# Recurrence: four of seven groups turned by DMA in pairs of tiles, eps added on VectorE, another order within a slot

## The chip, the cores and the metric

The kernel runs on one core of one Trainium2 chip. The metric is the device time of one execution in microseconds. The kernel before took 1867.72 us in the median of 3 runs (1865.54 to 1868.72).

## The reference, cut to what matters

There are 3327 rows of 256 values. Two graph attention layers and a mixture of experts come first, and then a recurrence of 30 steps over all rows. The change lies in the recurrence alone:

```python
def step(h, _):
    h = h + 0.01 * jnp.tanh(h)
    h = h * jax.nn.sigmoid(h)
    h = _layernorm(h, ln_w, ln_b)
    h = jnp.einsum('bsc,dc->bsd', h, W) + b
    return (h, None)
x, _ = jax.lax.scan(step, x, None, length=N_ITERS)     # N_ITERS = 30
...
x = x + _L1_ffn_ref((_layernorm(x, axis=-1))[None], ...)[0]
```

Each row goes through its 30 steps on its own; no row needs another. All of it is in float32.

## The kernel before

The rows lie in on-chip memory (SBUF) as 26 tiles of 128 rows by 256 values, `x`. In the recurrence the tiles are worked in seven groups: groups 0 to 5 have four tiles, group 6 has two. A "group" in the code is one group in one step, counted on through all steps, so `at` runs from 0 to 209, `at % 7` is the group and `at // 7` the step. Below, "group 3" means `at % 7 == 3`.

Within one step a group passes through these stages, each a method of the class `Group`:

- `tanh` (L1050, ScalarE): tanh of the state, one instruction for the group.
- `add` (L1053, GpSimd, called POOL in the profile): adds the state to it, one instruction, both operands in SBUF.
- `silu` (L1057, ScalarE): writes `z`.
- `measure` (VectorE, DVE in the profile): per tile the statistics (`bn_stats`, L1062) and their aggregate (`bn_aggr`, L1065), which give the variance.
- `invert` (GpSimd): adds eps to the variance (L1070) and raises it to the power -1/2 (L1071), 128 by 4 values.
- The turning of `z`: the product takes it with the 256 features along the partitions. `turn_here` does it on TensorE: two transposes for each tile (L1081) into PSUM, and a ScalarE copy for each pair of tiles out of PSUM (L1083). `turn_away` does it by DMA, on 16-bit halves: a ScalarE copy splits each float into its two halves (L1090, `parts`), a DMA writes them to DRAM (L1091, `apart`), and a transposing DMA reads them back (L1095, `zTa`). Both DMAs are issued by SyncE (SP). Groups 1, 3 and 5 go away, the others are turned here.
- `product` (TensorE, L1105): two matrix products for each tile against the 256x256 weight `wc`, into PSUM (`po`, two buffers). The profile shows each product as two MATMUL records.
- `evict` (VectorE, L1115): scales by the inverse deviation, adds the bias, and writes the new state, one instruction for each tile. One of its inputs lies in PSUM, the other, `bb`, in SBUF. In the last step it also adds the state kept from before the recurrence (L1122 loads it, L1123 adds it) and sends the rows out.

The loop at the end of the kernel is a software pipeline written out by hand. One turn of it is called a slot here. In a slot, group `at` is multiplied, while groups ahead of it pass through earlier stages; from the second step on the order of the instructions within each engine is exactly the order of the calls. Each engine works its own queue in order, so what a call waits for holds up what comes after it on that engine only.

```python
for at in range(-6, LAST + 2):
    on(at - 1, Group.evict)
    live.pop(at - 1, None)
    on(at + 3, Group.invert)
    on(at + 4, Group.silu)
    on(at + 2, lambda g: g.away or g.turn_here())
    on(at + 4, lambda g: g.away and g.turn_away())
    on(at + 4, Group.measure)
    on(at + 6, Group.tanh)
    on(at + 5, Group.add)
    on(at, Group.product)
```

So in one slot VectorE evicts group `at - 1` and measures group `at + 4`; GpSimd inverts `at + 3` and adds `at + 5`; ScalarE does silu and, for a group that goes away, `parts` of `at + 4`, or the copies of `at + 2`, and then tanh of `at + 6`; TensorE transposes `at + 2` and multiplies `at`. The tanh of `at + 6` needs the eviction of `at - 1` (the same rows, one step earlier) from the same slot. Buffers: `th` 3, `z` 4, `zT` 2, `parts` and `zTa` 2 each, DRAM `apart` 2.

The first attention layers use a large matrix of edges in SBUF, `adjT`, which is read for the last time (L281, VectorE, two SBUF inputs) just before the recurrence. Some of the recurrence's first stages for the first groups run beside that second attention stage.

Of the kernel before, what the change touches and what calls it, by code (L numbers as in the profile page):

```python
# [11 lines left out]
F32 = mybir.dt.float32  # L12
I32 = mybir.dt.int32
I16 = mybir.dt.int16
BF16 = mybir.dt.bfloat16
FP8 = mybir.dt.float8e4
AF = mybir.ActivationFunctionType
ALU = mybir.AluOpType
# [3 lines left out]
P = 128  # L22
ALPHA = 0.2
EPS = 1e-5
N_STEPS = 30
S = 100.0
G = 4
# [4 lines left out]
def gat_moe_gat_recurrent_ffn(ctx: ExitStack, tc: tile.TileContext, a: dict, out: bass.AP):  # L32
    nc = tc.nc
    N, D = a["x"].shape
    KD = D // P
    NT = (N + P - 1) // P
    NP = NT * P
    PAIRS = NT // 2
# [145 lines left out]
    class Scores:  # L184


        def __init__(self, pool, heads, s=None):
            self.s = pool.tile([P, NT, 2, heads], F32, name="s") if s is None else s
            self.row = pool.tile([P, NT, heads], F32, name="row")
            self.full = pool.tile([P, NT, heads], F32, name="full")  # L190
            self.part = pool.tile([P, NT, heads], F32, name="part")
            self.minus = pool.tile([P, NT, heads], F32, name="minus")
# [113 lines left out]
    graph = ctx.enter_context(tc.tile_pool(name="graph", bufs=1))  # L306
    adj_pairs = graph.tile([P, PAIRS, NP], BF16, name="adjT")
    adjT = adj_pairs.bitcast(FP8).rearrange("p c (i b) -> p c i b", b=2)
# [37 lines left out]
    dram = ctx.enter_context(tc.tile_pool(name="dram", bufs=1, space=bass.MemoryType.DRAM))  # L346
# [35 lines left out]
    with ExitStack() as moe:  # L382
# [447 lines left out]
        def product(hT, w):  # L830

            p = bank().rearrange("p (f q) -> p f q", f=FH)
            for f in range(FH):
                for k in range(KD):
                    nc.tensor.matmul(  # L835
                        p[:, f, :], lhsT=w[:, k, f * P : (f + 1) * P], rhs=hT[:, k, :],
                        start=(k == 0), stop=(k == KD - 1),
                    )
            return p
# [108 lines left out]
    narrow = ctx.enter_context(tc.tile_pool(name="narrow", bufs=8))  # L948
# [74 lines left out]
    with ExitStack() as st:  # L1023
        ps_t = st.enter_context(tc.tile_pool(name="ps3t", bufs=2, space=PSUM))
        turns = cycle((ps, ps_t))
        ps_o = st.enter_context(tc.tile_pool(name="ps3o", bufs=2, space=PSUM))
        last_p = st.enter_context(tc.tile_pool(name="last", bufs=2))

        apart = [dram.tile([G * P, 2, D], I16, name=f"apart{q}") for q in range(2)]
        apart_p = st.enter_context(tc.tile_pool(name="apart", bufs=2))  # L1030

        AWAY = (1, 3, 5)
        COUNT = len(groups)
        LAST = N_STEPS * COUNT

        class Group:

            def __init__(self, at):
                self.at = at
                self.ts = groups[at % COUNT]  # L1040
                self.n = len(self.ts)
                self.hs = x[:, self.ts[0] : self.ts[0] + self.n, :]
                self.away = at % COUNT in AWAY and at > 1

            def put(self, ins):
                return tc.keep_in_program_order(ins) if self.at >= COUNT else ins

            def tanh(self):
                self.th = steps["th"].tile([P, G, D], F32, name="th")[:, : self.n, :]
                self.put(nc.scalar.activation(self.th, self.hs, AF.Tanh, scale=1.0 / S))  # L1050

            def add(self):
                self.put(nc.gpsimd.tensor_tensor(self.th, self.th, self.hs, ALU.add))  # L1053

            def silu(self):
                self.z = steps["z"].tile([P, G, D], F32, name="z")[:, : self.n, :]
                self.put(nc.scalar.activation(self.z, self.th, AF.Silu, scale=1.0 / S))  # L1057

            def measure(self):
                stats = narrow.tile([P, G, 6], F32, name="stats")  # L1060
                for j in range(self.n):
                    self.put(nc.vector.bn_stats(stats[:, j, :], self.z[:, j, :]))  # L1062
                self.v = narrow.tile([P, G, 2], F32, name="v")
                for j in range(self.n):
                    self.put(nc.vector.bn_aggr(self.v[:, j, :], stats[:, j, :]))  # L1065

            def invert(self):
                self.r = narrow.tile([P, G], F32, name="rr")
                r = self.r[:, : self.n]
                self.put(nc.gpsimd.tensor_scalar(r, self.v[:, : self.n, 1], EPS, None, op0=ALU.add))  # L1070
                self.put(nc.gpsimd.tensor_tensor(r, r, neg_half[:, : self.n], ALU.pow))  # L1071

            def turn_here(self):
                pool = next(turns)
                zT = steps["zT"].tile([P, G, KD, P], F32, name="zT")
                for c in range(self.n // 2):
                    pt = pool.tile([P, 2, KD, P], F32, name="bank")
                    for j in range(2):
                        for k in range(KD):
                            (tc.keep_in_program_order if self.at > 1 else lambda ins: ins)(  # L1080
                                nc.tensor.transpose(pt[:, j, k, :], self.z[:, 2 * c + j, k * P : (k + 1) * P], ident)  # L1081
                            )
                    self.put(nc.scalar.copy(zT[:, 2 * c : 2 * c + 2, :, :], pt))  # L1083
                self.zT = lambda j, k: zT[:, j, k, :]

            def turn_away(self):
                n = self.n
                parts = apart_p.tile([P, G, 2, D], I16, name="parts")[:, :n]
                here = apart[self.at % COUNT // 2 % 2][: n * P]
                self.put(nc.scalar.copy(parts, self.z.bitcast(I16).rearrange("p j (d b) -> p j b d", b=2)))  # L1090
                nc.sync.dma_start(  # L1091
                    here.rearrange("(j p) b d -> p j (b d)", p=P), parts.rearrange("p j b d -> p j (b d)")
                )
                zT = apart_p.tile([P, KD, G * P], F32, name="zTa")
                nc.sync.dma_start(  # L1095
                    zT.bitcast(I16)[:, :, : n * 2 * P], here.rearrange("t b d -> (t b) d"), transpose=True
                )
                self.zT = lambda j, k: zT[:, k, j * P : (j + 1) * P]

            def product(self):  # L1100
                self.po = ps_o.tile([P, G, D], F32, name="po")
                for j in range(self.n):
                    for k in range(KD):
                        tc.keep_in_program_order(
                            nc.tensor.matmul(  # L1105
                                self.po[:, j, :], lhsT=self.zT(j, k), rhs=wc[:, k, :],
                                start=(k == 0), stop=(k == KD - 1),
                            )
                        )

            def evict(self):
                ts, n = self.ts, self.n
                for j in range(n):
                    self.put(
                        nc.vector.scalar_tensor_tensor(  # L1115
                            self.hs[:, j, :], self.po[:, j, :], self.r[:, j : j + 1], bb, op0=ALU.mult, op1=ALU.add
                        )
                    )
                if self.at >= LAST - COUNT:
                    here = slice(ts[0] * P, (ts[-1] + 1) * P)  # L1120
                    old = last_p.tile([P, G, D], F32, name="old")
                    nc.sync.dma_start(old[:, :n, :], kept[here, :].rearrange("(t p) d -> p t d", p=P))  # L1122
                    nc.vector.scalar_tensor_tensor(  # L1123
                        self.hs, self.hs, 1.0 / S, old[:, :n, :], op0=ALU.mult, op1=ALU.add
                    )
                    move_pairs(out, self.hs, ts[0] // 2, (ts[-1] + 1) // 2, True)

        live = {}

        def on(at, *what):  # L1130
            if 0 <= at < LAST:
                if at not in live:
                    live[at] = Group(at)
                for w in what:
                    w(live[at])

        for at in range(-6, LAST + 2):
            on(at - 1, Group.evict)
            live.pop(at - 1, None)
            on(at + 3, Group.invert)  # L1140
            on(at + 4, Group.silu)
            on(at + 2, lambda g: g.away or g.turn_here())
            on(at + 4, lambda g: g.away and g.turn_away())
            on(at + 4, Group.measure)
            on(at + 6, Group.tanh)
            on(at + 5, Group.add)
            on(at, Group.product)


# [47 lines left out]
```

## Time and profile before

| | us |
|---|---|
| median of 3 runs | 1867.72 |
| profiled execution, whole | 1862.0 |
| its span | 1860.3 |
| second attention stage: start of its last matmul (L286) | 1082.9 |
| recurrence, steady steps | 25.51 to 25.52 each |
| stretch from the start of the last step's products (1826.89) to the end | 33.41 |

The page gives busy time for each engine over the whole span (PE is TensorE's matmul, PEld its weight load, DVE VectorE, ACT ScalarE, POOL GpSimd). Inside the recurrence these shares are different from those of the whole, so the stretch of one step has to be asked for by itself. Durations of one instruction in the recurrence, from the groups by line between 1140 and 1820 us:

| line | engine | what | mean ns |
|---|---|---|---|
| L1050 | ACT | tanh, four tiles / two | 1060 / 639 |
| L1053 | POOL | add, four tiles / two | 2366 / 1278 |
| L1057 | ACT | silu, four tiles / two | 1052 / 613 |
| L1062 | DVE | statistics, one tile | 413 |
| L1065 | DVE | aggregate, one tile | 155 |
| L1070 | POOL | eps, four tiles | 229 |
| L1071 | POOL | power, four tiles / two | 1038 / 716 |
| L1083 | ACT | copy of two turned tiles | 576 |
| L1090 | ACT | parts of four tiles | 1900 |
| L1115 | DVE | evict, one tile | 475 |

Instructions of one engine overlap at their ends, so two in a row take less than the sum: four evictions take 1.66 us together, four statistics 1.41 us.

The longest waits in the same stretch, over its 26.6 steps, are all short: ScalarE's silu for GpSimd's add 69.1 us in 106 waits (longest 1.6), VectorE's eviction for TensorE 60.8 us in 106 (longest 1.1) and for GpSimd's `rr` 35.4 us in 27 (longest 1.3). TensorE has no wait in the list.

### The profile page before, as it was taken

How to read it: one execution, taken by the hardware profiler on the slowest of the kernel's cores; microseconds unless marked ns; L12 is line 12 of the kernel's file. 1: busy time of each engine (PE TensorE's matmuls, PEld its weight loads, DVE VectorE, ACT ScalarE, POOL GpSimd, SP SyncE). 2: the span in 40 equal slices, each digit the busy share in tenths (PEclk: the TensorE clock that was granted, in tenths of full speed). 3: DMA queues.
4: the chain of work that ended last, by engine and by line, in shares of the span. 5: the costliest groups of instructions: out<-in, count | busy, mean ns of one | idle time of the engine just before them, and what ended most of it. 6: DMA issues, size and time to landing. Idle time of an engine off the chain costs nothing.

```text
span 1860.3 us, 32198 instructions
## 1 busy us (share of the span) xinstructions
PE 1809.2 (97%) x11212; PEld 1653.9 (89%) x11212; DVE 1284.7 (69%) x3829; ACT 1186.9 (64%) x1498; POOL 939.3 (50%) x864
## 2 busy tenths in 40 slices
PE   7999999999999998899999999999999999999997
PEld 6999999998999998688888888888888888888886
DVE  7888888852222222666776778888888888888887
ACT  2877777641111111556666678888888888888884
POOL 3010212255333331101111159999999999999994
PEclk9999999999999999999999999999999999999999
DMA  8898260169999885400000035554555455555557
GB/s 175 114 122 99 57 100 22 61 224 298 339 338 336 298 284 166 151 14 17 21 15 17 17 108 125 124 127 125 118 132 117 123 133 125 121 121 125 125 127 202
DMA packets 377309, 253.97 MB, mean 137 GB/s; under 512 B 238821, under 2 KB 336924, under 8 KB 377146
## 3 DMA queue, kind: packets, MB, share of 16 engines
q1 hardware_dynamic: 361026, 219.04, 43.1%
q0 software_dynamic: 11440, 28.09, 8.8%
q10 hardware_dynamic: 4680, 4.76, 0.8%
q8 instruction: 91, 1.49, 0.3%
q14 instruction: 72, 0.59, 0.1%
HBM read 168.19 MB, written 76.49 MB: 132 GB/s over the span
## 4 chain that ended last, share of the span: by engine, by line
PE 67%; issue 10%; DVE 6%; POOL 5%; DMA 5%; ACT 0%; SPq 0%; POOLq 0%; DVEq 0%; ACTq 0%
PE po L1105 35%; PE acc L286 24%; PE bank L1081 5%; DVE pT L281 3%; POOL given L855 2%; POOL rb L761 2%; DMA given<-wh,to 2%; DMA wh<-in_w_dram 1%; DMA old<-kept 1%; DMA lists<-pair,ati 1%; PE bank L835 1%; PE acc L163 1%; PE bank L526 1%; POOL rstd L121 1%; PE bank L148 0%
## 5 line engine op out<-in xcount | busy, mean ns | idle before, releaser
L276 ACT ACTIVATE e<-rb,minus,full 128x384 f32<-128x384 f32 (+3 forms) x494 | 400.1, 823 | 166.7 <-DVE pT L281 150.6
L1053 POOL TENSOR_TENSOR th<-th,x 128x1024 f32<-128x1024 f32 (+1 forms) x210 | 465.1, 2215 | 16.0 <-ACT th L1050 14.4
L281 DVE SCALAR_TENSOR_TENSOR pT<-e,part,adjT 128x384 f32<-128x384 f32 (+3 forms) x494 | 383.3, 780 | 118.8 <-PE acc L286 103.4
L1115 DVE SCALAR_TENSOR_TENSOR x<-po,rr,bb 128x256 f32<-128x256 f32 x780 | 323.0, 475 | 104.2 <-PE po L1105 67.3
L1105 PE MATMUL po<-wc,zT 128*128 128x256 f32 x1696 | 385.9, 379 | 1.2 <-DVE x L1115 1.2
L1105 PEld LDWEIGHTS po<-wc,zT 128*128 128x128 f32 x1696 | 315.1, 190 | 40.7 <-issue 1.6
L1105 PE MATMUL po<-wc,zTa 128*128 128x256 f32 x1424 | 321.9, 379 | 0.0
L286 PE MATMUL acc<-wh,pT 128*128 128x129 f32 x2704 | 309.8, 276 | 2.1 <-DVE pT L281 2.1
L286 PEld LDWEIGHTS acc<-wh,pT 128*128 128x128 f32 x2704 | 305.0, 192 | 2.7 <-DVE pT L281 2.5
L1105 PEld LDWEIGHTS po<-wc,zTa 128*128 128x128 f32 x1424 | 268.3, 190 | 35.3
L286 PE MATMUL acc<-s_wh,pT 128*128 128x257 f32 x1352 | 295.2, 381 | 3.5 <-DVE pT L281 3.3
L286 PEld LDWEIGHTS acc<-s_wh,pT 128*128 128x128 f32 x1352 | 256.0, 190 | 42.1 <-DVE pT L281 6.3
L1062 DVE BATCH_NORM_STATS2 stats<-z 128x6 f32<-128x256 f32 x780 | 275.1, 413 | 20.7 <-ACT z L1057 20.6
L1057 ACT ACTIVATE z<-th 128x1024 f32<-128x1024 f32 (+1 forms) x210 | 207.9, 990 | 76.9 <-POOL th L1053 76.7
L121 POOL TENSOR_TENSOR rstd<-ve,neg_half 128x4 f32<-128x4 f32 (+3 forms) x28 | 30.8, 1101 | 409.5 <-DVE ve L119 326.1
L1050 ACT ACTIVATE th<-x 128x1024 f32<-128x1024 f32 (+1 forms) x210 | 209.8, 1000 | 27.0 <-DVE x L1115 24.1
L1071 POOL TENSOR_TENSOR rr<-rr,neg_half 128x4 f32<-128x4 f32 (+1 forms) x210 | 208.4, 992 | 17.5
L1090 ACT COPY parts<-z 128x2048 int16<-128x2048 int16 x89 | 169.1, 1900 | 5.9 <-PE acc L286 4.0
L881 ACT ACTIVATE e<-bank 128x512 f32<-128x512 f32 x61 | 36.4, 597 | 196.3 <-PE bank L835 183.5
L885 DVE TENSOR_TENSOR pT<-e,bank 128x512 f32<-128x512 f32 x61 | 41.9, 688 | 167.5 <-PE bank L835 167.4
L835 PEld LDWEIGHTS bank<-hT,wh 128*128 128x128 f32 x1280 | 149.3, 192 | 4.9 <-ACT hT L827 1.4
L835 PE MATMUL bank<-hT,wh 128*128 128x128 f32 x1280 | 150.5, 275 | 2.4 <-DMA wh<-in_w_dram 2.4
(196 smaller groups left out, 1640.0 us busy)
## 6 DMA issues: line engine op xcount, KB each, us to landing
wh<-in_w_dram SPq DMA_DIRECT2D x120, 512.0 KB
apart<-parts SPq DMA_DIRECT2D x89, 512.0 KB
first_set<-in_w_dram SPq DMA_DIRECT2D x63, 512.0 KB
in_bytes<-in_adj_dram POOLq DMA_DIRECT2D x3, 2496.0 KB, 28.7
x<-in_x_dram SPq DMA_DIRECT2D x6, 512.0 KB
kept<-x SPq DMA_DIRECT2D x8, 384.0 KB
old<-kept SPq DMA_DIRECT2D x6, 512.0 KB
out_dram<-x SPq DMA_DIRECT2D x6, 512.0 KB
```

The source lines that it names most:

```text
L276: nc.scalar.activation(e[:, : n * P], rb[:, : n * P], AF.Relu, scale=sc.full[:, j, h : h + 1], bias=sc.minus[:, j, h : h + 1],)
L281: masked = nc.vector.scalar_tensor_tensor(pT[:, : n * P], e[:, : n * P], sc.part[:, j, h : h + 1], adjT[:, j // 2, ts[0] * P : (ts[-1] + 1 ...
L286: nc.tensor.matmul(po[c], lhsT=pT[:, c * P : (c + 1) * P], rhs=wh[:, j, h, :], start=(j == 0 and c % per_bank == 0), stop=(j == NT - 1), s ...
L835: nc.tensor.matmul(p[:, f, :], lhsT=w[:, k, f * P : (f + 1) * P], rhs=hT[:, k, :], start=(k == 0), stop=(k == KD - 1),)
L1050: self.put(nc.scalar.activation(self.th, self.hs, AF.Tanh, scale=1.0 / S))
L1053: self.put(nc.gpsimd.tensor_tensor(self.th, self.th, self.hs, ALU.add))
L1057: self.put(nc.scalar.activation(self.z, self.th, AF.Silu, scale=1.0 / S))
L1062: self.put(nc.vector.bn_stats(stats[:, j, :], self.z[:, j, :]))
L1071: self.put(nc.gpsimd.tensor_tensor(r, r, neg_half[:, : self.n], ALU.pow))
L1090: self.put(nc.scalar.copy(parts, self.z.bitcast(I16).rearrange("p j (d b) -> p j b d", b=2)))
L1105: nc.tensor.matmul(self.po[:, j, :], lhsT=self.zT(j, k), rhs=wc[:, k, :], start=(k == 0), stop=(k == KD - 1),)
L1115: nc.vector.scalar_tensor_tensor(self.hs[:, j, :], self.po[:, j, :], self.r[:, j : j + 1], bb, op0=ALU.mult, op1=ALU.add)
```

## The change

Group 0 goes away too. The round trip through DRAM is split into `send_away` and `take_back`, each in pairs of tiles, so that every DMA and every `parts` copy has half its size, and the two calls stand in different slots. The buffers of the round trip move into the place of `adjT`, which is dead by then: three for `parts`, five for what comes back, and four in DRAM. All DMAs of the round trip are kept in program order. Eps is added by VectorE at the end of `measure`, straight into `rr`, and GpSimd's `invert` keeps the power alone. Within a slot, silu is called one group further ahead (`at + 5`), measure, the transposes here and the power at other distances, and all calls in another order.

```diff
-        apart = [dram.tile([G * P, 2, D], I16, name=f"apart{q}") for q in range(2)]
-        apart_p = st.enter_context(tc.tile_pool(name="apart", bufs=2))
-
-        AWAY = (1, 3, 5)
+        apart = cycle([dram.tile([G * P, 2, D], I16, name=f"apart{q}") for q in range(4)])
+        space = graph.tile([P, PAIRS, NP], BF16, name="adjT").rearrange("p c n -> p (c n)").bitcast(F32)
+        spaces = [space[:, i * G * D : (i + 1) * G * D] for i in range(8)]
+        room_parts, room_back = cycle(spaces[:3]), cycle(spaces[3:])
+
+        AWAY = (0, 1, 3, 5)
...
+                self.r = narrow.tile([P, G], F32, name="rr")
+                self.put(
+                    nc.vector.tensor_scalar(self.r[:, : self.n], self.v[:, : self.n, 1], EPS, None, op0=ALU.add)
+                )
 
             def invert(self):
-                self.r = narrow.tile([P, G], F32, name="rr")
                 r = self.r[:, : self.n]
-                self.put(nc.gpsimd.tensor_scalar(r, self.v[:, : self.n, 1], EPS, None, op0=ALU.add))
                 self.put(nc.gpsimd.tensor_tensor(r, r, neg_half[:, : self.n], ALU.pow))
...
-            def turn_away(self):
-                n = self.n
-                parts = apart_p.tile([P, G, 2, D], I16, name="parts")[:, :n]
-                here = apart[self.at % COUNT // 2 % 2][: n * P]
-                self.put(nc.scalar.copy(parts, self.z.bitcast(I16).rearrange("p j (d b) -> p j b d", b=2)))
-                nc.sync.dma_start(
-                    here.rearrange("(j p) b d -> p j (b d)", p=P), parts.rearrange("p j b d -> p j (b d)")
-                )
-                zT = apart_p.tile([P, KD, G * P], F32, name="zTa")
-                nc.sync.dma_start(
-                    zT.bitcast(I16)[:, :, : n * 2 * P], here.rearrange("t b d -> (t b) d"), transpose=True
-                )
-                self.zT = lambda j, k: zT[:, k, j * P : (j + 1) * P]
+            def send_away(self):
+                halves = self.z.bitcast(I16).rearrange("p j (d b) -> p j b d", b=2)
+                parts = next(room_parts).bitcast(I16).rearrange("p (j b d) -> p j b d", b=2, d=D)
+                self.sent = next(apart)
+                for c in range(0, self.n, 2):
+                    self.put(nc.scalar.copy(parts[:, c : c + 2], halves[:, c : c + 2]))
+                    tc.keep_in_program_order(
+                        nc.sync.dma_start(
+                            self.sent[c * P : (c + 2) * P].rearrange("(j p) b d -> p j (b d)", p=P),
+                            parts[:, c : c + 2].rearrange("p j b d -> p j (b d)"),
+                        )
+                    )
+
+            def take_back(self):
+                back = next(room_back).rearrange("p (c k t) -> p c k t", c=2, k=KD)
+                for c in range(0, self.n, 2):
+                    tc.keep_in_program_order(
+                        nc.sync.dma_start(
+                            back[:, c // 2].rearrange("p k t -> p (k t)").bitcast(I16)
+                            .rearrange("p (k t) -> p k t", k=KD),
+                            self.sent[c * P : (c + 2) * P].rearrange("t b d -> (t b) d"), transpose=True,
+                        )
+                    )
+                self.zT = lambda j, k: back[:, j // 2, k, j % 2 * P : (j % 2 + 1) * P]
...
         for at in range(-6, LAST + 2):
+            on(at + 4, lambda g: g.away and g.send_away())
             on(at - 1, Group.evict)
             live.pop(at - 1, None)
-            on(at + 3, Group.invert)
-            on(at + 4, Group.silu)
-            on(at + 2, lambda g: g.away or g.turn_here())
-            on(at + 4, lambda g: g.away and g.turn_away())
-            on(at + 4, Group.measure)
             on(at + 6, Group.tanh)
+            on(at + 1, Group.invert)
             on(at + 5, Group.add)
+            on(at + 3, Group.measure)
             on(at, Group.product)
+            on(at + 3, lambda g: g.away and g.take_back())
+            on(at + 5, Group.silu)
+            on(at + 3, lambda g: g.away or g.turn_here())
```

The condition that a group goes away only from `at > 1` on stands as before, so in the first step group 0 and group 1 are turned here.

## The prediction

> **What bounds the kernel now.** I read the page first, for its span, the shares of the engines and the chain that ended last.
>
> ```profile
> span 1860.3 us, 32198 instructions
> PE 1809.2 (97%) x11212; PEld 1653.9 (89%) x11212; DVE 1284.7 (69%) x3829; ACT 1186.9 (64%) x1498; POOL 939.3 (50%) x864
> PE 67%; issue 10%; DVE 6%; POOL 5%; DMA 5%; ACT 0%; SPq 0%; POOLq 0%; DVEq 0%; ACTq 0%
> ```
>
> TensorE leads, but these are averages over four stages, and the change touches only the last. So I asked for the chain within one step of the recurrence (start, length, what), and for the busy time of each engine in that step (columns: stretch, its length, PE, PEld, DVE, ACT, POOL, granted clock, DMA share, GB/s).
>
> ```profile
> 1393.16 6.91 PE po L1105 x32
> 1400.08 0.87 PE bank L1081 x8
> 1400.95 6.91 PE po L1105 x32
> 1407.86 0.44 PE bank L1081 x4
> 1408.29 3.46 PE po L1105 x16
> 1411.75 0.87 PE bank L1081 x8
> 1412.62 5.18 PE po L1105 x24
> 1417.81 0.87 PE bank L1081 x8
> 1393.16:1418.68 25.52, 25.52 (x134) 22.64 (x133) 21.27 (x79) 21.98 (x25) 23.74 (x22) 1.00 0.52 124
> ```
>
> The chain is TensorE without a gap: 22.46 us of products and 3.05 of transposes make the 25.52 of the step. The clock is full. A step gets shorter only if TensorE has less to do, and then only as far as the others follow, and they are close behind: POOL 23.74, ACT 21.98, DVE 21.27. The steps at both ends of the stage (1112.52 and 1801.38) also take 25.51, so one step stands for all.
>
> **What the Trainium skill says, and whether the trace agrees.** "SBUF — State Buffer", section "SBUF: two separate sides", says that VectorE and GpSimd share one pair of SBUF ports under an exclusive lock: a VectorE instruction in a two-port mode, or with two SBUF inputs, and a GpSimd one exclude each other for the whole instruction. "VectorE: DVE Perf Modes", section "Mode 2×_2P — use both read ports for one tensor", says that a float32 tensor_scalar from SBUF to SBUF runs at twice the rate by reading through both ports. The new eps instruction is of that kind, so it should take the lock. The trace agrees on the rate (a 128x256 tensor_scalar with an immediate took 284 ns at L820, one with a column operand at L816 406), and on the lock for two-input instructions:
>
> ```profile
> 899.66 0.61 DVE L281 SCALAR_TENSOR_TENSOR pT<-e,part,adjT 128x384 f32<-128x384 f32 x1
> 900.06 2.42 POOL L1053 TENSOR_TENSOR th<-th,x 128x1024 f32<-128x1024 f32 x1 [1.94 <-ACT th L1050]
> 900.63 2.80 DVE L281 SCALAR_TENSOR_TENSOR pT<-e,part,adjT 128x384 f32<-128x384 f32 x2 [0.36 <-ACT e L276]
> 776.05 1.01 POOL L121 TENSOR_TENSOR rstd<-ve,neg_half 128x4 f32<-128x4 f32 x1 [1.85 <-DVE ve L119]
> 776.61 0.15 DVE L198 TENSOR_SCALAR minus<-part 128x4 f32<-128x4 f32 x1
> 777.02 0.17 DVE L119 TENSOR_SCALAR ve<-mv 128x4 f32<-128x4 f32 x1
> ```
>
> L281 takes 0.61 us alone, but two of them beside the GpSimd add ended at 903.43, 0.95 after the add: the first had waited. The last three lines show small tensor_scalars inside a GpSimd power, not held. So the add blocks and the power doesn't. That the add blocks a tensor_scalar no line here shows. The third page is "DMA: Bandwidth & Descriptors", section "Anatomy of one DMA — SWDGE (gpsimd) path": most of a DMA's fixed cost of about 2 us is the receipt at the end, worst into HBM. Its figure is for another issuing path; here, from SP, 2.99 us lie between the issue of a `parts` write and that of the transpose that waits for it:
>
> ```profile
> 1400.74 0.38 SPq L1091 DMA_DIRECT2D apart<-parts  x1
> 1403.73 2.18 SPq L1095 DMA_TRANSPOSE zTa<-apart  x1
> 1407.00:1407.50 0.50, 0.50 (x4) 0.42 (x4) 0.50 (x4) 0.33 (x1) 0.50 (x1) 1.00 0.77 173
> 1407.50:1408.00 0.50, 0.50 (x5) 0.42 (x4) 0.30 (x5) 0.35 (x1) 0.26 (x2) 1.00 0.01 1
> ```
>
> SP is done with that transpose at 1405.91, and the DMA share (last column but one) falls to 0.01 after 1407.50: the data is there about 1.55 us after SP's part.
>
> **The change part by part.**
>
> *Group 0 away.* Removed: eight transposes on TensorE, 0.87 us a step, in the 29 steps from the second on (in the first, group 0 stays): 29 x 0.87 = 25.2 us. TensorE's step becomes 25.52 - 0.87 = 24.65. Removed from ACT: two copies, 0.94 us (in a row they start 0.47 apart).
>
> *Parts in halves.* A float instruction of 1024 elements takes ACT 1.05 us and the next starts 0.955 after it; 2048 take 1.90 and 1.81. I take 0.955 for each half. So 8 x 0.955 - 3 x 1.81 = 2.2 us more; ACT: 21.98 + 2.2 - 0.9 = 23.3 of 24.65.
>
> *Eps.* GpSimd loses seven times 0.23: 23.74 - 1.6 = 22.1. VectorE gains seven of about 0.16 (L119, the same shape, takes 0.157): 21.27 + 1.1 = 22.4. Bounds: nothing below that, since L119 is the same instruction; above it, each may wait for a running add, up to 2.37 us.
>
> *DMA.* Share 0.52 of 25.52 is 13.3 us for three groups, 4.4 each; four make 17.7 of 24.65, or 0.72. SP: half a transpose costs between half of the median 2.26 and all of it; 1.5 is taken.
>
> *The order.* All engines now lie between 22 and 23.3 us beneath TensorE's 24.65, so queues must not wait on each other badly. I laid one step out on TensorE's clock, 0 being the start of group 0's product, adding the durations along each queue in the new order, 0.04 us for a signal. Example: product 0 ends at 3.62; evict 0 starts at 3.66 and keeps DVE 1.58, the statistics of group 4 1.31, their aggregates 0.36, so eps comes at 6.93. ACT does parts of group 5 from 4.39 to 6.39, then tanh of group 0 to 7.34; GpSimd, done with its power, starts the add of group 0 at 7.38. In all seven slots eps comes at 0.87, 3.42, 6.93, 10.39, 13.88, 18.18 and 22.07, and the next add starts at 0.89, 4.23, 7.38, 10.72, 14.24, 18.81 and 22.15. Eps falls into the power each time, though twice by less than 0.1 us. Behind a held eps stand the next eviction and with it tanh, the add and silu; TensorE waits only when `po`, two buffers, isn't evicted. DVE has 24.65 - 22.4 = 2.25 us a step to spare, so one block of that length is hidden.
>
> *Moved waits.* Of the away groups, 0 and 1 are the tight pair, for group 0's transposes stand in SP's queue behind group 1's writes. Group 1's parts end at 17.8; its second write leaves SP by 18.3, and four half transposes follow. Group 0's first is there at 18.3 + 1.5 + 1.55 = 21.4, needed at 24.65; group 1's last at 18.3 + 6.0 + 1.55 = 25.9, needed when two tiles of its product are done, 28.1 + 1.73 = 29.8. At 2.26 each it is 28.9, still in time. The new buffers take waits away (L1095 waited 78.6 us for TensorE to free `zTa`), which cost nothing before. `adjT` is free only after the last L281, but the first parts waited until 1083.29 before too. The silu further ahead needs a fourth live `z`, which exists.
>
> *The ends.* The first step and the last stretch keep their makeup. That stretch, 33.41 us, hangs on the loads of `old`, issued by SP between other DMAs; two half transposes now stand there in place of one of 3.38. I put it at 0, bounds -2 and +2.
>
> The sum: 1862.0 - 25.2 = 1836.8 us for the profiled execution. The median of the runs lies 5.7 us above that execution, and I carry this over: 1867.72 - 25.2 = 1842.5 us.
>
> **The rivals.**
>
> *Held at two thirds or less* (an engine becomes the bound). ACT at 23.3 of 24.65 has 1.35 us, and its work is lumpy: 4.8 us in the slot with group 3's parts and group 2's copies, where TensorE takes 2.6. If the slots average 25.1, the gain is 29 x 0.4 = 12 us: 1856. For it: every engine is above 90%. Against it: POOL has 93% now and costs TensorE no wait.
>
> *The lock decides: slower.* If eps arrives while an add runs in two slots of a step, VectorE pays about 2.2 us each: 22.4 + 4.4 = 26.8 us, 1.3 above the step now, or 29 x 1.3 = 38 us: 1905. The point from which it is slower is 25.52 - 22.4 = 3.1 us blocked in a step. If every slot were caught, eviction, tanh, add and eps would follow each other, 1.66 + 1.06 + 2.37 + 0.16 = 5.3 us a slot, far worse. For it: the add runs 15.5 of 24.65 us, two margins are thin, and a delayed eviction lets GpSimd run empty, so that the next add starts as soon as tanh ends. Against it: ACT's and GpSimd's own backlog puts the add behind eps, and one held eps fits into the slack.
>
> *The round trip arrives late.* A half transpose would have to cost over 2.5 us on SP, more than a whole one does. At 3 us group 1's second half comes 2.0 us late in each step, and the gain turns into 29 x (2.0 - 0.87) = 33 us of loss: 1900. It also stands for the change not doing what it says.
>
> **How the numbers follow.** The forecast, 1842.5, gets 0.70, with a range of its own of 1838 to 1847. The partial gain, about 1856, gets 0.12. The lock gets 0.13, the late round trip 0.02, and 0.03 goes to a gain that is given back to within the measurement. About 0.2% of the time, 3.7 us, is what a measurement of this kernel can tell from no change. So faster 0.70 + 0.11 = 0.81, a little of the partial gain being too small to count; same 0.04; slower 0.15. The range from 1834 to 1866 takes in the forecast with the bounds of the ends and nearly all of the partial gain, 0.82 in all.
>
> **What would show it.** Right: steps of 24.65 us with TensorE busy throughout, three groups of L1081 left in a step, ACT near 23.3, DVE near 22.4 and POOL near 22.1, and eps at about 0.16 us. The lock would show as eps instructions of 1 to 2.4 us and TensorE waiting for VectorE's evictions; a late round trip as TensorE waiting for DMA; ACT as the bound, as waits for `z` or tanh. The prediction is wrong if a step isn't within 0.15 us of 24.65.

## The result, and the profile after

The changed kernel took 1840.36 us in the median of 4 runs (1839.59 to 1841.14), beside 1868.11 us for the kernel before on the same chip: a ratio of 0.9857, with a 95% interval from 0.9846 to 0.9869. The forecast was 1842.5 us. The profiled execution took 1841.14 us.

First the page of the changed kernel, its span, the busy time of each engine and the shares of the chain that ended last:

```profile
span 1839.4 us, 32502 instructions
PE 1787.4 (97%) x10980; PEld 1631.7 (89%) x10980; DVE 1319.1 (72%) x4039; ACT 1223.9 (67%) x1587; POOL 888.4 (48%) x654
PE 67%; issue 10%; DVE 6%; POOL 5%; DMA 3%; ACT 1%; another core or an unknown queue 0%; SPq 0%; POOLq 0%; DVEq 0%; ACTq 0%
```

The page alone hardly shows a change: PE still has 97%. One step of the recurrence does. This is the chain of waits inside it (start, length, what), and the busy time in two steps (columns as before: stretch, length, PE, PEld, DVE, ACT, POOL, clock, DMA share, GB/s):

```profile
1394.68 6.91 PE po L1120 x32
1401.59 0.44 PE bank L1085 x4
1402.03 8.64 PE po L1120 x40
1410.66 0.87 PE bank L1085 x8
1411.54 6.91 PE po L1120 x32
1418.44 0.87 PE bank L1085 x8
```

```profile
1402.03:1426.66 24.63, 24.63 (x125) 21.80 (x125) 22.35 (x86) 23.27 (x27) 21.94 (x15) 1.00 0.73 172
1426.66:1451.30 24.64, 24.64 (x126) 21.80 (x125) 22.42 (x86) 23.27 (x27) 21.93 (x15) 1.00 0.66 171
```

TensorE is still the whole chain, without a gap. Three groups of transposes are left in a step, 0.87 + 0.44 + 0.87 us, where there were four, and the step is 24.64 us instead of 25.52. The other engines stand where the sum put them, ScalarE closest with 23.27.

What hung on timing was eps. From the timeline of the changed kernel, eps (L1070) and GpSimd's power (L1075) and add (L1055), with start, length and, in brackets, the idle time before and what ended it:

```profile
1411.28 1.03 POOL L1075 TENSOR_TENSOR rr<-rr,neg_half 128x4 f32<-128x4 f32 x1
1412.33 0.17 DVE L1070 TENSOR_SCALAR rr<-v 128x4 f32<-128x4 f32 x1
1412.41 2.38 POOL L1055 TENSOR_TENSOR th<-th,x 128x1024 f32<-128x1024 f32 x1
1414.75 1.01 POOL L1075 TENSOR_TENSOR rr<-rr,neg_half 128x4 f32<-128x4 f32 x1
1414.91 0.17 DVE L1070 TENSOR_SCALAR rr<-v 128x4 f32<-128x4 f32 x1
1415.74 1.28 POOL L1055 TENSOR_TENSOR th<-th,x 128x512 f32<-128x512 f32 x1
1418.38 0.17 DVE L1070 TENSOR_SCALAR rr<-v 128x4 f32<-128x4 f32 x1
1419.00 2.37 POOL L1055 TENSOR_TENSOR th<-th,x 128x1024 f32<-128x1024 f32 x1 [1.01 <-ACT th L1052]
```

Eps takes 0.17 us each time, inside a power (1414.91) or ahead of an add, at the narrowest by 0.08 us. In the first step of the same kernel one came later than that, and it waited until the add had ended (1099.69 + 2.36 = 1102.05; 1100.77 + 1.32 = 1102.09):

```profile
1099.69 2.36 POOL L1055 TENSOR_TENSOR th<-th,x 128x1024 f32<-128x1024 f32 x1 [1.75 <-ACT th L1052]
1100.77 1.32 DVE L1070 TENSOR_SCALAR rr<-v 128x2 f32<-128x2 f32 x1
```

So the lock exists for this instruction, and the steady step misses it by its timing alone. That made the lock the main rival to test, beside the question of which part of the change carries the gain.

### The profile page after: what moved, and what is told of

It reads as the page before. It is cut to its first block, busy times and chain, and to the rows that moved or that the text cites. A ratio compares the mean times of both kernels' runs of the same rounds, so it can differ in the third digit from the quotient of the medians.

```text
span 1839.4 us, 32502 instructions
## 1 busy us (share of the span) xinstructions
PE 1787.4 (97%) x10980; PEld 1631.7 (89%) x10980; DVE 1319.1 (72%) x4039; ACT 1223.9 (67%) x1587; POOL 888.4 (48%) x654
## 4 chain that ended last, share of the span: by engine, by line
PE 67%; issue 10%; DVE 6%; POOL 5%; DMA 3%; ACT 1%; another core or an unknown queue 0%; SPq 0%; POOLq 0%; DVEq 0%; ACTq 0%
PE po L1120 35%; PE acc L286 24%; PE bank L1085 4%; DVE pT L281 3%; POOL given L855 2%; POOL rb L761 2%; DMA given<-wh,to 2%; PE bank L835 1%; PE acc L163 1%; PE bank L148 1%; DMA old<-kept 1%; PE bank L526 1%; PE acc L851 1%; DMA lists<-pair,ati 0%; DVE x L1130 0%
## 5 line engine op out<-in xcount | busy, mean ns | idle before, releaser
L1055 POOL TENSOR_TENSOR th<-th,x 128x1024 f32<-128x1024 f32 (+1 forms) x210 | 465.0, 2214 | 94.1 <-ACT th L1052 86.4
L1120 PE MATMUL po<-wc,adjT 128*128 128x256 f32 x1888 | 422.2, 379 | 0.0
L1120 PEld LDWEIGHTS po<-wc,adjT 128*128 128x128 f32 x1888 | 356.4, 190 | 47.6 <-DVE x L1130 0.3
L1130 DVE SCALAR_TENSOR_TENSOR x<-po,rr,bb 128x256 f32<-128x256 f32 x780 | 325.1, 478 | 61.8 <-PE po L1120 61.2
L1120 PE MATMUL po<-wc,zT 128*128 128x256 f32 x1232 | 281.0, 379 | 0.8 <-DVE x L1130 0.8
L1120 PEld LDWEIGHTS po<-wc,zT 128*128 128x128 f32 x1232 | 229.2, 190 | 29.7 <-issue 1.1
L1095 ACT COPY adjT<-z 128x1024 int16<-128x1024 int16 x236 | 235.2, 1044 | 4.8 <-DVE pT L281 2.0
L1052 ACT ACTIVATE th<-x 128x1024 f32<-128x1024 f32 (+1 forms) x210 | 209.2, 996 | 29.0 <-DVE x L1130 23.8
L1075 POOL TENSOR_TENSOR rr<-rr,neg_half 128x4 f32<-128x4 f32 (+1 forms) x210 | 206.8, 985 | 26.4 <-DVE rr L1070 26.3
```

Of the source, the lines that this page charges most:

```text
L1095: self.put(nc.scalar.copy(parts[:, c : c + 2], halves[:, c : c + 2]))
L1120: nc.tensor.matmul(self.po[:, j, :], lhsT=self.zT(j, k), rhs=wc[:, k, :], start=(k == 0), stop=(k == KD - 1),)
L1130: nc.vector.scalar_tensor_tensor(self.hs[:, j, :], self.po[:, j, :], self.r[:, j : j + 1], bb, op0=ALU.mult, op1=ALU.add)
```

## The experiments

The twelve ran on three chips, four on each, on which the kernel before took 1861.5 to 1861.8 us; each ratio is to the kernel before on the same chip. Step lengths below are the distances between the tanh instructions of group 0 in each trace; "held" is what eps instructions took beyond their time alone (0.17 us, from a column 0.23), summed over a step.

| run | median us | ratio to before (95%) | steady step, us | eps held in a step, us |
|---|---|---|---|---|
| the changed kernel again | 1834.75 | 0.9854 (0.9838 to 0.9871) | 24.64 | 0.0 to 0.1 |
| three groups away | 1903.15 | 1.0220 (1.0196 to 1.0244) | 25.80 and 28.06 | 6.4 in two steps |
| kernel before, four away | 1847.52 | 0.9919 (0.9895 to 0.9942) | 24.82 to 25.7, mean 25.0 | on GpSimd |
| eps on GpSimd | 1836.70 | 0.9870 (0.9849 to 0.9892) | 24.62 | on GpSimd |
| old order | 1845.07 | 0.9915 (0.9893 to 0.9937) | 24.92 | 1.2 |
| three away, eps on GpSimd | 1861.02 | 0.9996 (0.9987 to 1.0005) | 25.51 | on GpSimd |
| three away, eps from a column | 1906.64 | 1.0244 (1.0224 to 1.0264) | 25.81 and 28.06 | 5.9 in two steps |
| eps late | 1851.86 | 0.9950 (0.9931 to 0.9969) | 25.10 | 3.7 |
| kept rows loaded early | 1838.81 | 0.9877 (0.9861 to 0.9894) | 24.64 | 0.0 to 0.1 |
| both: eps on GpSimd, rows early | 1833.56 | 0.9852 (0.9835 to 0.9868) | 24.63 | on GpSimd |
| five away, in halves | 1850.40 | 0.9943 (0.9924 to 0.9963) | 25.16 | on GpSimd |
| five away, parts whole | 1839.59 | 0.9885 (0.9868 to 0.9901) | 24.69 | on GpSimd |

**Three groups away**, everything else as changed.

```diff
-        AWAY = (0, 1, 3, 5)
+        AWAY = (1, 3, 5)
```

> The changed kernel with group 0 turned on TensorE again (groups 1, 3 and 5 away); order, halves, eps on VectorE and buffers stay as changed. Theory (the whole gain is the eight transposes a step that leave TensorE, the rest only makes room): steps of 25.52 us again, about 1865.6 us (1840.4 + 25.2), within 2 us of the kernel before. Rival (the new order, the earlier silu or the lighter GpSimd carry part of the gain): steps under 25.3 us, under 1860 us.

Neither came. The kernel became 2.2% slower than the one before, with steps of 25.80 and 28.06 us by turns. The timeline of a long step of this run shows why (DVE's L1130 is the eviction, ACT's L1052 tanh, POOL's L1055 the add; `adjT` in a product's line is the room that `z` comes back to):

```profile
1389.39 2.36 POOL L1055 TENSOR_TENSOR th<-th,x 128x1024 f32<-128x1024 f32 x1 [1.70 <-ACT th L1052]
1389.78 1.99 DVE L1070 TENSOR_SCALAR rr<-v 128x4 f32<-128x4 f32 x1
1391.69 1.65 DVE L1130 SCALAR_TENSOR_TENSOR x<-po,rr,bb 128x256 f32<-128x256 f32 x4
1393.37 1.06 ACT L1052 ACTIVATE th<-x 128x1024 f32<-128x1024 f32 x1 [2.65 <-DVE x L1130]
1393.39 3.72 PE L1120 MATMUL po<-wc,adjT 128*128 128x256 f32 x16 [0.80 <-DVE x L1130]
1394.57 2.35 POOL L1055 TENSOR_TENSOR th<-th,x 128x1024 f32<-128x1024 f32 x1 [1.70 <-ACT th L1052]
1394.96 1.98 DVE L1070 TENSOR_SCALAR rr<-v 128x4 f32<-128x4 f32 x1
```

The add starts 0.39 us before eps, and eps is over only when the add is. Behind it in VectorE's queue stands the eviction, about 1.8 us late with it; tanh waits 2.65 us for the eviction, GpSimd runs dry for 1.70 us, and so the next add starts as soon as tanh is done, again 0.39 us before eps. One turn of this ring is 1394.96 - 1389.78 = 5.18 us, where TensorE's work for a slot is about 3.5 to 4.3, so TensorE waits for the eviction (0.80 us here). The busy times say the same, for 28.06 us of a long step and, counted from group 6's product to the next, for the short step after it (25.51 us on TensorE's clock, 25.80 from tanh to tanh):

```profile
1378.28:1406.34 28.06, 26.00 (x133) 22.25 (x132) 27.67 (x85) 20.37 (x26) 20.25 (x13) 1.00 0.46 99
1406.51:1432.02 25.51, 25.51 (x133) 22.66 (x132) 22.61 (x85) 23.66 (x30) 23.45 (x16) 1.00 0.51 131
```

In the first DVE is the full engine, 27.67 of 28.06, of which some 5.8 us is waiting inside eps. In the second TensorE is.

**Three away with eps on GpSimd**, to see whether the lock is all of it.

```diff
         AWAY = (1, 3, 5)
...
-                self.put(
-                    nc.vector.tensor_scalar(self.r[:, : self.n], self.v[:, : self.n, 1], EPS, None, op0=ALU.add)
-                )
             def invert(self):
+                self.r = narrow.tile([P, G], F32, name="rr")
                 r = self.r[:, : self.n]
+                self.put(nc.gpsimd.tensor_scalar(r, self.v[:, : self.n, 1], EPS, None, op0=ALU.add))
                 self.put(nc.gpsimd.tensor_tensor(r, r, neg_half[:, : self.n], ALU.pow))
```

> The changed kernel with three groups away (1, 3, 5) and eps on GpSimd again; otherwise as in the three-group run, which had steps of 25.80 and 28.06 us by turns and eps instructions of up to 2.0 us. Theory (VectorE's eps is held by GpSimd's add, and nothing else slows that run): steps of 25.52 us throughout, within 0.2% of the kernel before. Rival (the run is slow because group 0's copies wait for a zT buffer or because of the order): steps still alternate, mean 26.9 us, 2% slower than before.

The theory held: 25.51 us in the steady steps, and a time that can't be told from the kernel before. One of these steps:

```profile
1373.04:1398.55 25.51, 25.51 (x133) 22.64 (x132) 21.14 (x80) 22.29 (x29) 23.65 (x22) 1.00 0.52 124
```

So eps on VectorE is the whole loss of the run above, 42 us; and the new order, the halves, the earlier silu and the new buffers together gain nothing while the eight transposes are there.

**Four away with eps on GpSimd** (the same edit on the changed kernel).

> The changed kernel with eps added by GpSimd again, just ahead of its power. Theory (TensorE is the bound): GpSimd has 21.9 + 7 x 0.23 = 23.5 us of work in a step of 24.65, steps stay at 24.65 us, 1840 us within 2. Rival (eps on VectorE is needed, for GpSimd's queue is lumpy and full at 95%): steps of 24.9 us or more, over 1848 us, and TensorE or VectorE waits for rr.

The theory held again. The busy times of a step of this run:

```profile
1382.09:1406.72 24.63, 24.63 (x126) 21.80 (x125) 21.13 (x79) 23.05 (x28) 23.65 (x22) 1.00 0.67 168
```

POOL at 23.65 of 24.63 costs nothing. This run and the one before it differ in group 0 alone: 1861.02 - 1836.70 = 24.3 us in the medians (of two chips, on which the kernel before took 1861.6 and 1861.5), 25.51 - 24.62 = 0.89 us a step. That is what turning group 0 away gains with the rest of the change in place, nearly all of the gain, and moving eps was not needed for it.

**Three away, eps from a column**: the same place, but the constant read from SBUF.

```diff
-                    nc.vector.tensor_scalar(self.r[:, : self.n], self.v[:, : self.n, 1], EPS, None, op0=ALU.add)
+                    nc.vector.tensor_scalar(self.r[:, : self.n], self.v[:, : self.n, 1], eps_col[:, 0:1], None, op0=ALU.add)
```

> The three-group run again with eps on VectorE in the same place, but read from a column in SBUF instead of an immediate. Theory (it is the form that reads through both ports that is held): eps at about 0.2 us throughout, steps of 25.5 us, within 0.2% of the kernel before. Rival (any VectorE instruction that comes while GpSimd adds is held, or this form needs the ports too): eps of up to 2 us and steps of 25.8 and 28.06 us as with the immediate, 2% slower than before.

The theory fell, the rival held:

```profile
1392.62 2.36 POOL L1057 TENSOR_TENSOR th<-th,x 128x1024 f32<-128x1024 f32 x1 [1.70 <-ACT th L1054]
1393.01 2.00 DVE L1072 TENSOR_SCALAR rr<-v,eps_col 128x4 f32<-128x4 f32 x1
```

The column form takes 0.23 us alone and is held just the same. "Any VectorE instruction" goes too far, though, as the next run shows. Why the column form is held, by a second port for the same tensor or by a second input in SBUF, stays open.

**Eps late**, in the changed kernel, after the evictions of the next slot.

```diff
+            on(at + 2, Group.add_eps)
             on(at + 3, Group.measure)
```

> The changed kernel (four groups away) with eps taken from the end of the statistics to the next slot, right after the evictions, where by the slot table most of the adds are running. Theory (the lock has a price, and in the changed kernel only the timing avoids it): eps of 1 to 2 us in several slots of each step, together over the 2.25 us that VectorE has to spare, steps of 25.4 us or more, at least 20 us over the changed kernel, no better than before. Rival (the lock matters only with three groups away): eps stays near 0.17 us or hides, steps 24.65 us, 1.4% faster than before.

The lock has its price here too, but a smaller one than expected: 25.10 us a step, +0.46, and the kernel stayed ahead of the one before. From its timeline (L1132 is the eviction, L1072 eps):

```profile
1406.80 1.63 DVE L1132 SCALAR_TENSOR_TENSOR x<-po,rr,bb 128x256 f32<-128x256 f32 x4
1407.17 2.37 POOL L1055 TENSOR_TENSOR th<-th,x 128x1024 f32<-128x1024 f32 x1 [1.09 <-ACT th L1052]
1408.34 1.22 DVE L1072 TENSOR_SCALAR rr<-v 128x4 f32<-128x4 f32 x1
```

The eviction goes on at its own speed beside the same add that holds eps until 1409.5: only eps is held. And eps now stands behind the eviction, so tanh isn't held up with it and the ring of the three-group run does not close. Held time of 3.7 us a step against 2.25 us to spare should have cost 1.5; it cost 0.46, the time that TensorE waits for an eviction once a step. DVE is busy for 24.90 of 25.10 us here, 2.5 more than in the changed kernel and not 3.7, since the recorded lengths of neighbours overlap.

**The old order**, with the halves, the buffers and eps of the changed kernel.

> The changed kernel with the calls of a slot in the order and at the distances of the kernel before; the take back follows the sending in the same slot. Theory (the order matters little so long as TensorE is the bound): steps of 24.65 us, 1840 us within 3. Rival (the new order is what lets the engines follow): steps of 25 us or more, over 1850 us.

In between: 24.92 us. Eps is held for 1.2 us a step (the longest takes 0.99 us), and TensorE's weight loads (PEld) wait for an eviction once a step, 6.6 us in 25 waits. From the timeline, and from the waits between 1140 and 1780 us:

```profile
1387.66 2.36 POOL L1055 TENSOR_TENSOR th<-th,x 128x1024 f32<-128x1024 f32 x1
1389.55 0.50 DVE L1070 TENSOR_SCALAR rr<-v 128x4 f32<-128x4 f32 x1
PEld po L1120 <- DVE x L1130: 6.6, 25, 0.6
```

The chain of waits inside a step no longer goes through TensorE but round through ScalarE, GpSimd and VectorE, and of the held eps only this one, held for 0.33 us, lies on it. That is about what a step loses, so the two probably belong together, but no run has this order with eps on GpSimd. So with eps on VectorE the order is worth about 0.28 us a step, 8 us in 29 steps.

**The kernel before with group 0 away as well**, nothing else but a DRAM buffer for each away group.

```diff
-        AWAY = (1, 3, 5)
+        AWAY = (0, 1, 3, 5)
...
-                here = apart[self.at % COUNT // 2 % 2][: n * P]
+                here = apart[AWAY.index(self.at % COUNT)][: n * P]
```

> The kernel before with group 0 away as well and a DRAM buffer for each away group; old order, whole-group transfers, eps on GpSimd, two buffers each for parts and what comes back. Theory (removing the transposes is enough, since every engine stays under 24.65 us a step: POOL 23.74, ACT 21.98 - 0.94 + 1.81 = 22.9, DVE 21.3): steps of 24.65 to 24.8 us, 1840 to 1846 us. Rival (without the new order and buffers the engines cannot follow and TensorE waits): steps over 25.1 us, over 1853 us.

Neither bound was met: 1847.52 us, more than half of the steps at 24.82, the others up to 25.7, and 25.0 in the mean. The timeline of a long step of this run, with SP's queue:

```profile
1407.88 0.57 SPq L1091 DMA_DIRECT2D apart<-parts  x1
1411.48 2.22 SPq L1095 DMA_TRANSPOSE zTa<-apart  x1
1416.33 1.97 PE L1105 MATMUL po<-wc,zTa 128*128 128x256 f32 x8 [0.85 <-DMA zTa<-apart]
```

With whole transfers and each transpose right behind its own write in SP's queue, a group comes back 0.85 us late: the late round trip. The change puts an end to it, and not by taking back in another slot: with the old order, where each group's transposes follow its own writes in the same slot, TensorE waited for no DMA either. Halves and buffers were not separated. Nor is the late round trip the whole loss: between 1140 and 1780 us a quarter of this run's chain of waits lies on GpSimd, and only 3% on the transposing DMA. Even so, this small edit alone brings more than half of the gain, 0.8% of 1.4%; the rest of the change, which gains nothing while group 0 is turned on TensorE, brings the other 10.8 us to four away with eps on GpSimd.

**The kept rows loaded early.** The end of the changed kernel's chain stands on loads of `old` (two shown), which SP issues one group at a time behind the rows going out:

```profile
1822.00 7.73 DMA old<-kept
...
1831.56 3.38 DMA old<-kept
```

The edit loads them in the fourth step into room that `adjT` leaves.

```diff
-                    old = last_p.tile([P, G, D], F32, name="old")
-                    nc.sync.dma_start(old[:, :n, :], kept[here, :].rearrange("(t p) d -> p t d", p=P))
+                    old = olds[self.at % COUNT]
...
+            on(at, lambda g: 3 * COUNT <= g.at < 4 * COUNT and g.load_old())
```

> The changed kernel with the rows kept for the last addition loaded in the fourth step into unused room, not one group at a time at the end. Theory (after the last step's products the chain of waits stands on these loads): the stretch from the last step's products to the end falls from 43.2 us by 3 to 6 us, steps stay at 24.64, so 0.2 to 0.3% less than the changed kernel, a ratio of about 0.983 to before. Rival (VectorE's own work ends the kernel there and the loads are hidden): under 1 us, a ratio of 0.986.

The end did shrink. From the start of group 4's product in the last step but one, the anchor of the 43.2 us, it is 43.34 us in the changed kernel and 40.19 here. But the kernel gained nothing, since it was 3.3 us slower from the first product to that anchor: two early steps took 26.63 and 27.84 us, from the same ring:

```profile
1120.71 2.35 POOL L1065 TENSOR_TENSOR th<-th,x 128x1024 f32<-128x1024 f32 x1 [1.70 <-ACT th L1054]
1121.10 1.99 DVE L1080 TENSOR_SCALAR rr<-v 128x4 f32<-128x4 f32 x1
```

This is before the loads were issued, so they did not set it off; a slightly different start of the recurrence is what remains, which no run separated. Here the ring opened again after two steps; with three groups away it closed anew in every second one.

**Both edits, five groups away, and the changed kernel beside them.**

> The changed kernel itself, once more, so that the next three can be set against it on one chip. Expected: steps of 24.64 us, a ratio to before of 0.986, as in the first comparison.

> The changed kernel with both edits that gave something or cost nothing: eps on GpSimd, and the kept rows loaded in the fourth step. Theory (the early load takes 3 us from the end, and its own run lost them again to eps instructions held in the first two steps, 6.0 us in one of them): with eps on GpSimd no step is longer than 24.7 us and the loss is gone, 3 to 6 us under the changed kernel, a ratio to before of 0.982 to 0.984. Rival (the load itself disturbs the first steps): early steps of over 26 us again, no faster than the changed kernel.

With eps on GpSimd the long early step is 26.12 us, yet from the first product (1084.2 in both) to group 4's product in the last step but one it takes 704.81 us, as the changed kernel does here (704.82), so nothing is lost. The end is 2.2 us shorter, 40.36 instead of 42.57. The medians differ by 1.2 us and their intervals overlap, so a gain is not shown, and 3 to 6 us were expected.

> The kernel of the run before with group 2 away as well (0, 1, 2, 3 and 5). Theory (ScalarE is next: 23.3 - 0.94 + 1.91 = 24.2 us of work a step, and lumpy): although TensorE falls to 23.77, steps do not get shorter than 24.65, 25.2 is likeliest, at least as slow as with four away. Rival (TensorE bounds all the way down): steps of 23.8 us, 25 us faster.

```diff
-        AWAY = (0, 1, 3, 5)
+        AWAY = (0, 1, 2, 3, 5)
```

The theory held, with 25.16 us for 25.2. ScalarE has about half of the chain of waits between 1140 and 1780 us, TensorE a quarter, and TensorE has gaps. From the timeline of its queue in this run:

```profile
1411.32 3.69 PE L1128 MATMUL po<-wc,adjT 128*128 128x256 f32 x16 [0.30 <-DMA adjT<-apart]
1415.45 3.69 PE L1128 MATMUL po<-wc,adjT 128*128 128x256 f32 x16 [0.44 <-DMA adjT<-apart]
```

> Five groups away as in the run before, with one parts copy for four tiles in place of two, the transfers still in halves. Theory (ScalarE is next): its work falls by 5 x 0.10 = 0.5 us to 23.7, and the step falls by about as much, to 24.6 to 24.8 us, close to four groups away. Rival (the DMA or SP is what limits five groups, share 0.72 x 5/4 = 0.90 of a step): no change from five in halves.

```diff
-                for c in range(0, self.n, 2):
-                    self.put(nc.scalar.copy(parts[:, c : c + 2], halves[:, c : c + 2]))
+                self.put(nc.scalar.copy(parts, halves))
+                for c in range(0, self.n, 2):
```

The step fell by 0.47 us to 24.69, as ScalarE's 0.5 us less asks for, while the bytes stayed the same. So what TensorE waits for as "DMA" most likely comes late because ScalarE's `parts` are late. Both runs also lost time once, 5.8 and 6.9 us, in the two steps where the kept rows are loaded between the transposes; five groups without that load was not run.

## Why the prediction was right

**The bound and the sum.** TensorE without a gap, less 0.87 us a step: 25.52 became 24.64, and 24.65 was forecast. From the first product to the end the profiled executions take 1860.3 - 1087.0 = 773.3 us before and 1839.4 - 1091.25 = 748.15 after, 25.15 us less where 29 x 0.87 = 25.2 was worked out; so the ends, put at 0, did stay. The medians differ by 27.75 us, and 25.2 lies within the interval (24.5 to 28.8). The rest, 2.6 us, need not come from the recurrence: its first product starts at 1091.25 in one execution of the changed kernel and at 1084.21 in another, on another chip, and that spread of the earlier stages is larger. For the same reason the 5.7 us carried over from the profiled execution to the median can't be said to have been right; it did no harm.

**What lies beside it.** ScalarE 23.27 (23.3 forecast), VectorE 22.4 (22.4), GpSimd 21.93 (22.1), DMA 0.66 to 0.73 (0.72). A half transpose takes SP 1.24 us in the median, where 1.5 was taken: a term that was too dear, without effect, since TensorE waits for no DMA.

**The slot table.** Counted from group 0's product (1411.54), eps comes at 0.79, 3.37 and 6.84 us and the adds at 0.87, 4.20 and 7.46; the table had 0.87, 3.42, 6.93 and 0.89, 4.23, 7.38. The other four slots agree as well, to 0.1 us. Two margins of under 0.1 us were forecast and are there. But one of them was 0.02 us in a table that is off by up to 0.1, so that eps would come first in that slot could not be known from it. That neither of its two traces shows the changed kernel in the ring is in part luck: with the kept rows loaded early the same loop was caught in two early steps.

**The lock.** It was given 0.13 and a price: two held eps a step, 26.8 us, 1905 us, and a ring of 5.3 us a slot if all are caught. The changed kernel escapes it, but the rival was no phantom: with three groups away the mean step is 26.93 us, the time 41.7 us above the kernel before, where 38 were worked out, and the ring 5.18 us. That 41.7 lies so near to 38 is chance, since 38 was for four groups away and 4.4 us held in each step. The sum against VectorE's 2.25 us to spare was too simple in both directions: 1.2 us held in the old order goes with 0.28 us lost, 3.7 us with 0.46, and on average 3.2 us with 1.4. By these traces what decides is whether an eviction stands behind the held instruction and the next add behind that eviction. "SBUF — State Buffer", section "SBUF: two separate sides", says that whichever of the two starts first keeps the ports for its whole instruction. The traces agree for the eps held by adds (2.36 us of add, eps of up to 2.0 us) and not for the power, inside which eps took 0.17 us. What the prediction took for agreement on the doubled rate was thin: its 406 ns for the column form is the mean of two instructions of 334 and 477 ns, and 284 isn't half of it.

**The other rivals.** The late round trip is real in whole transfers with the old buffers (0.85 us) and gone in the changed kernel. ScalarE as the bound was looked for with four groups; it comes with five.

## What to carry to other kernels

When one engine is busy without a gap, only work taken from that engine shortens the step; here halves, a new order and more buffers together were worth nothing by themselves and served to keep the other engines out of the way, and moving eps was not needed at all. An instruction moved onto a neighbour that shares ports must be placed on a timeline against what that neighbour runs, and with what queues behind it: an instruction of 0.17 us cost 42 us of 1861 where an eviction stood behind it. A timing that is free by 0.08 us is fragile, so take the placement that can't collide if it costs as little, as eps on GpSimd did here.

## What the runs showed of the hardware

- A tensor_scalar of 128x4 values on VectorE was held until the end of a running GpSimd add of two SBUF operands, in the steady steps for up to 1.8 us beyond its time alone, both with an immediate (1.99 us) and with a column operand (2.00 us, 0.23 alone).
- In the same slots the eviction (one tensor in PSUM, one in SBUF, and a column in SBUF) was not held: 1.63 us for four of them with an add running, 1.65 to 1.66 otherwise.
- GpSimd's power of two 128x4 operands (1.02 us) did not hold eps, which took 0.17 us inside it.
- Two states of one loop, 25.80 and 28.06 us by turns for 27 steps, came with one kind of instruction being held in some slots and not in others; the program is the same from step to step.
